# Two-layer convolution kernel: where the sines are computed, how the last channels of the first image are stored, and how the last image's tail is queued

## The chip, the cores and the metric

The kernel runs on one core of one Trainium2 chip. The metric is the device time of one execution in microseconds (us). Lower is better. Times of several runs are given as a median with their range.

## The reference, cut to what matters

The input x holds 8 images of 8 channels and 512 x 512 pixels in 32-bit floats. Two residual layers follow each other. Both normalise x over groups of two channels first.

```python
x = x + _L0_conv_ref(_gn(x), T, X, weights1_ri, weights2_ri)
x = x + _L1_conv_ref(_gn(x), K_local, Wp, bp, Wu, bu, Wg1, bg1, Wg2, bg2)
```

Layer 0 is spectral: it takes 32 low frequencies (8 in one direction, 4 in the other) of every second pixel, mixes the channels, and builds the image again from cosines and sines (`E1`, `E2`) whose arguments come from the vectors X and T. Layer 1 has three parts on its normalised input x:

```python
grid = drive                                    # drive = x
for _ in range(15):
    mapped = R * grid * (1.0 - grid)            # logistic map
    local = _conv(mapped, K_local, groups=8)    # 3x3, each channel by itself
    grid = 0.85 * (0.7 * mapped + 0.3 * local) + 0.15 * drive
cml_out = clip(grid, 0.0001, 0.9999)
nca_out = sigmoid(_conv(relu(_conv(x, Wp, bp)), Wu, bu))     # 3x3 to 128, 1x1 to 8
gin = concatenate([x, cml_out, nca_out])
g = sigmoid(_conv(relu(_conv(gin, Wg1, bg1)), Wg2, bg2))     # 3x3, 1x1
return g * cml_out + (1.0 - g) * nca_out
```

## The kernel before, in words

**Stages of an image.** The program calls an image an element. `layer0` (line 321) is a generator that does layer 0 and the normalisation of layer 1 in small pieces; each `yield` names the slot of the schedule in which the next piece may be put (wide, early, fill, late). It ends with `close` (line 414), which normalises a pair of channels and stores them to the DRAM plane `xn`. From `xn` three users read:

- `Slabs` and `Tail`: the 15 steps of the logistic map. A set is a tile of 128 partitions x 4 x 512. Each step is 48 matmuls from `convolve` (line 529), a VectorE addition (line 548) and a ScalarE square (line 554). Nine sets make an image: four for channels 0 to 3, four for channels 4 to 7, and the tail. Results go to the plane `cml`.
- `Hidden` (line 706): the 3x3 convolution to 128 channels, in 128 rounds of four image rows. A round is 24 matmuls (line 734) into four PSUM banks, which ScalarE empties for one half (line 740) and VectorE for the other (line 742). Its input tile `cols` serves four rounds and has two buffers; `Hidden.load` (line 714) issues the next one after every fourth round. `point` (line 757) does the 1x1 convolution; after every fourth round the result `y` goes to the plane `nca` (line 776), 16 rows at a time.
- `Gate` (line 783): 43 blocks of 12 rows. `load` (line 789) issues six DMAs (three for `gin`, three for `mix`), `conv` (line 806) needs 24 matmuls (line 811), a GpSimd subtraction (line 816), and two VectorE operations (lines 817 and 821). `point` (line 823) needs 6 matmuls (line 828), a sigmoid on ScalarE (line 832) and a GpSimd product (line 834). `finish` (line 836) adds on VectorE (line 839) and stores to `out` (line 846).

**Order.** Nothing is planned by a cost model. The order of the source is the order on every engine: `keep_order` (line 103) ties each instruction to the one before it on its engine. The unit of the schedule is a turn (line 1071), counted by `now`; `later(1, ...)` puts work off to the end of the turn. One turn, in `work` (line 1026), is: three map steps; `others.finish()` for the gates whose point was issued in the turn before; the transfers; up to three hidden rounds; the 1x1 sums; up to two gate convolutions; their points; the loads of new gates. While image b is mapped and convolved, the gates of image b-1 and layer 0 of image b+1 fill the gaps.

**The start.** Line 186 issues the loads of the eight channels of image 0. The loop of line 1004 then runs the pieces of its layer 0. At the piece with number 8, so after the statistics of all eight channels, it calls `sines` (line 224: three times a chain of seven VectorE instructions on 8 x 512 and a sine on ScalarE, then four small DMAs from ScalarE's queue) and `bands` (line 258: the weights of the map, 120 small GpSimd instructions). All of ScalarE's loads of constants and the stores of zero rows (lines 973 and 976) stand ahead of this in ScalarE's queue. As soon as four channels are stored, 16 loads (`first.load`, line 1018) of two of the four sets are issued. After the loop two `cols` loads follow (lines 1020 and 1021), and the other 16 set loads come from `Phase.fetch` (line 698) in the first turns. Eight rounds in three turns run before the first map step.

**The tail.** During the last image only 56 of its 128 rounds are done beside the map (line 54). What is left runs in the loop of line 1133: 72 rounds, three a turn, so 24 turns, and the 43 gates of this image. A turn loads two gates if at most four are loaded and waiting (line 1134). `Others.conv` (line 943) takes a gate if the turn has reached `hold` and the gate was loaded at least `lag` turns ago; line 1131 sets these to three turns from now and 2. In this tail the stores of `nca` go through GpSimd's queue, since `lag` is not 0 (line 776); the `cols` loads go through SyncE's queue (SP) like all other loads.

Of the kernel before, what the change touches and what calls it, by code (L numbers as in the profile page):

```python
# [41 lines left out]
P = 128  # L42
C = 8
N = 512
NS = N // 2
G = 4
# [19 lines left out]
assert TAIL_AT + TAIL_ROWS[0][1] == N - SLAB + TAIL_ROWS[1][0]  # L66
SLOTS, SHARED, MORE, LEAST = 19, 4, 7, 3
AHEAD = 12


MAGIC = 12582912.0
# [41 lines left out]
def view(t, offset, dims):  # L113

    return bass.AP(tensor=t.tensor, offset=t.offset + offset, ap=[list(d) for d in dims])
# [3 lines left out]
def conv_layers(ctx: ExitStack, tc: tile.TileContext, a, out):  # L119
    nc = tc.nc  # L120
# [42 lines left out]
    put_off, now = [], [0]  # L163

    def later(ticks, work):
        put_off.append((now[0] + ticks, work))
# [57 lines left out]
    def sines():  # L224
        u, k, t = (sets.take([8, N], name) for name in ("u", "k", "sines"))
        rd = sm.tile([8, 1], F32, name="rd")
        for to, name, col, shift in (
            (e1[:8], "X", 0, 0.25), (t, "X", 0, 0.0), (e2[:8], "T", 1, waves[:8, 2:3])
        ):
            xr = grid[name]  # L230
            nc.vector.tensor_tensor(rd, xr[:, 2:3], xr[:, 0:1], ALU.subtract)
            nc.vector.reciprocal(rd, rd)
            nc.vector.tensor_tensor(rd, rd, waves[:8, col : col + 1], ALU.mult)
            nc.vector.tensor_scalar(u, xr, rd, shift, ALU.mult, ALU.add)
            nc.vector.tensor_scalar(k, u, MAGIC, None, ALU.add)
            nc.vector.tensor_scalar(k, k, MAGIC, None, ALU.subtract)
            nc.vector.tensor_tensor(u, u, k, ALU.subtract)
            nc.scalar.activation(to, u, AF.Sin, scale=6.283185)
        nc.scalar.dma_start(out=e1[8:16], in_=t)
        for j in range(1, 4):  # L240
            nc.scalar.dma_start(out=e2[32 * j : 32 * j + 8], in_=e2[:8])
        for tile_ in (u, k, t, *grid.values()):
            sets.drop(tile_)
# [14 lines left out]
    def bands():  # L258
        nc.vector.tensor_scalar(kk, kk, -R * (1.0 - BETA) * EPS, None, ALU.mult)
        nc.vector.tensor_scalar(  # L260
            kk[:, 4::9], kk[:, 4::9], -R * (1.0 - BETA) * (1.0 - EPS), None, ALU.add
        )
        for c in range(C):
            for dx in range(3):
                to = band[:, c, dx]
                for dy in range(3):
                    at = c * 9 + dy * 3 + dx
                    nc.gpsimd.tensor_scalar(
                        part if dy else to, shift[:, dy], kk[:, at : at + 1], None, ALU.mult
                    )  # L270
                    if dy:
                        nc.gpsimd.tensor_tensor(to, to, part, ALU.add)
        ky = prep[:, 192 : 192 + C * 3].rearrange("p (c y) -> p c y", y=3)
        nc.vector.tensor_reduce(ky, kk.rearrange("p (c y x) -> p c y x", y=3, x=3), AX.X, ALU.add)
        full = prep[:, 224 : 224 + C]
        nc.vector.tensor_reduce(full, ky, AX.X, ALU.add)
        nc.vector.tensor_scalar(full, full, -0.25, -0.5, ALU.mult, ALU.add)
        nc.vector.tensor_scalar(ky, ky, 0.25, None, ALU.mult)
        nc.vector.tensor_copy(base[:, :, 1], full)
        for e, (j, dy) in enumerate(((0, 0), (2, 2), (3, 0), (4, 2))):  # L280
            nc.vector.scalar_tensor_tensor(
                base[:, :, j], ky[:, :, dy], ends[:, e : e + 1], full, ALU.mult, ALU.add
            )
        for c in range(C):
            at = slice(32 * (c % 4), 32 * (c % 4) + 32)
            nc.vector.tensor_copy(base_e[at, c // 4], base[at, c, 0:3])
        nc.vector.tensor_copy(base[64:, 0:4, 4], base[64:, 4:8, 4])
# [33 lines left out]
    def layer0(e, bank):  # L321
# [6 lines left out]
        for c in range(C):  # L328
            yield (LATE if c % 2 else EARLY), c
            xt = e.x[c]  # L330
# [61 lines left out]
        to = om[:16, :C]  # L392
# [21 lines left out]
        def close(g, mv):  # L414

            mean, rstd, std = yield from group_stats(mv, 1, bank)
            nc.vector.tensor_copy(means[:, 0, g : g + 1], mean)
            nc.vector.tensor_copy(means[:, 1, g : g + 1], std)
            for c in (2 * g, 2 * g + 1):
                xt = e.x[C + c]  # L420
                nc.vector.tensor_scalar(xt, xt, mean, rstd, ALU.subtract, ALU.mult)

                def store(c=c, xt=xt):
                    nc.sync.dma_start(
                        out=e.xn[1 : N + 1, c].rearrange("(p j) w -> p j w", j=4), in_=xt
                    )
                    e.done_with(C + c)
                    e.closed.append(c)

                later(1, store)  # L430

        def synthesis(ty, xt, half):
            ps, at = bank[-1], slice(2 * half, 2 * half + 2)
# [233 lines left out]
    class Phase:  # L667
# [23 lines left out]
        def squares(self, n):  # L691
            while self.squared < len(self.sets) and sets.room():
                if not self.ready(self.squared, 0, n + TICK):
                    break
                self.sets[self.squared].square()
                self.squared += 1

        def fetch(self, n):
            while n - self.at >= -AHEAD and self.loads:
                s, _, h = self.loads[0]  # L700
# [5 lines left out]
    class Hidden:  # L706
# [7 lines left out]
        def load(self):  # L714
            assert len(self.e.closed) == C
            t = wk.tile([P, 2, N], F32, tag="cols", name="cols", bufs=2)
            nc.sync.dma_start(
                out=t,
                in_=view(
                    self.e.xn, 16 * self.loaded * C * N, [[N, P], [2 * C * N, 2], [1, N]]  # L720
                ),
            )
            self.loaded += 1
            self.tiles.append(t)
# [58 lines left out]
    class Gate:  # L783
# [60 lines left out]
        def store(self):  # L844
            lo = self.first - self.r0
            nc.sync.dma_start(
                out=view(
                    out, self.e.b * C * N * N + self.first * N,
                    [[N, GR - lo], [N * N, C], [1, N]],
                ),  # L850
                in_=self.mix[C * lo : GR * C, 1],
            )
            shared.drop(self.mix)
# [115 lines left out]
    for i in range(3):  # L969
        xn = dram.tile([NP + 1, C, N], F32, name=f"xn{i}")  # L970
        cml, nca = (dram.tile([NP, C, N], F32, name=f"{name}{i}") for name in ("cml", "nca"))
        for plane in (xn, cml, nca):
            nc.scalar.dma_start(
                out=view(plane, 0, [[(NP - 1) * C * N, 2], [N, C], [1, N]]), in_=zrow
# [24 lines left out]
    e = element(0)  # L999
# [2 lines left out]
    turns = cycle(pairs)  # L1002
    others = Others()
    for n in count():
        if n == C:
            sines()
            bands()
        if not e.pieces:
            break
        ps = next(turns)  # L1010
        e.spectral(e.need[0], ps if e.need[0] == WIDE else ps[:, 0])
        tick()

        first = phases[0]
        while (
            len(e.closed) >= C // 2 and len(first.loads) > 8 * (SETS - 2) and sets.room()
        ):
            first.load()
    tick(end=True)
    e.hidden.load()  # L1020
    e.hidden.load()

    halves = pairs[:2], pairs[2:]
    used = [0]

    def work(steps, rounds, e, after, gates, transfers, squares=lambda: None):

        def half():
            used[0] += 1
            return halves[used[0] % 2]  # L1030

        settled = iter(())
        for n, (s, step) in enumerate(steps):
            ps = half()
            s.convolve(step, ps)
            next(settled, None)
            settled = s.settle(step, ps)
            next(settled)
            others.finish()
            if gates == 2:  # L1040
                others.load(1)
                gates = 1
        others.finish()
        transfers()
        for _ in range(rounds):
            e.hidden.round(half(), after, settled)
        next(settled, None)
        squares()


        first, second = halves[used[0] % 2], halves[(used[0] + 1) % 2]
        if not others.spectral(WIDE, second):
            used[0] += 1
            first, second = second, first
        groups = e.hidden.sums()
        if len(groups) == 2:
            e.hidden.point(groups.pop(0), first[1][:, 0])
        others.conv(first[0][:, 0])
        others.spectral(EARLY, [second[0][:, 0]])
        two = others.conv(second[0][:, 0])  # L1060
        if groups:
            e.hidden.point(groups[0], first[1][:, 1])
        others.spectral(FILL, [None])
        others.spectral(LATE, [second[1][:, 0], second[0][:, 0]])
        others.point()
        used[0] += two
        others.load(gates)
        tick()
        squares()
# [24 lines left out]
    for b in range(B):  # L1094
        e = elements[b]
# [3 lines left out]
        first, second = phases[2 * b : 2 * b + 2]  # L1099
# [28 lines left out]
        others.mapped.append(e)  # L1128


    others.after, others.hold, others.lag = None, now[0] + 3, 2
    sets.most = shared.most = SLOTS
    while e.hidden.n < ROUNDS or others.mapped or others.busy():
        turn(at, min(TICK, ROUNDS - e.hidden.n), e, None, 2 if len(others.loaded) <= 4 else 0)
# [57 lines left out]
```

## Time and profile before

| what | us |
|---|---|
| three runs, median (range) | 9339.16 (9327.55 to 9340.95) |
| profiled execution, its time | 9328.59 |
| profiled execution, its span | 9326.8 |
| first round of the hidden convolution begins | 138.0 |
| first map step begins | 175.4 |
| tail begins (first of its 24 turns) | 8838.3 |
| last hidden round's sums end | 9283.7 |
| last VectorE addition of a gate begins | 9322.1 |

Times inside the profile count from the start of the span. Engines are PE (matmul), PEld (its weight loads), DVE (VectorE), ACT (ScalarE), POOL (GpSimd) and SP (SyncE, which only issues DMAs here); a name with q is the engine's queue of instructions that issue or wait. In a row of groups the numbers behind the bar are busy time and mean nanoseconds of one, then the idle time just before and what ended it. In the timeline a bracket gives the idle time before the row and its releaser. In the table of stretches each engine has its busy time and number of instructions, then come TensorE's granted clock, the mean busy share of the 16 DMA engines and GB/s. PE is busy for 94% of the span, with the granted clock at 0.987 on average.

### The profile page before, as it was taken

The numbers are of one execution on the slowest core, as the hardware profiler recorded it, in microseconds if no ns is written. First come the engines' busy times: TensorE is split into PE (matmuls) and PEld (weight loads), VectorE is DVE, ScalarE is ACT, GpSimd is POOL, SyncE is SP. The second block draws the span as 40 slices with busy tenths as digits, with TensorE's granted clock in tenths as the row PEclk, the third lists the DMA queues.
The fourth block names the chain that finished last, engine by engine and source line by source line (L and its number), as shares of the span: only waits on it lengthen the run. The fifth ranks groups of instructions, "written<-read, shape, count | busy, mean of one in ns | idle before, by whom it ended". The sixth has DMA issues, their size and how long they took to land. (4 is left out here: it accounts for less than half of the span.)

```text
span 9326.8 us, 334742 instructions
## 1 busy us (share of the span) xinstructions
PE 8776.0 (94%) x150992; PEld 4165.1 (45%) x150992; DVE 5685.6 (61%) x5844; ACT 4101.0 (44%) x4285; POOL 3378.9 (36%) x4441
## 2 busy tenths in 40 slices
PE   5999999999999999999999999999999999899988
PEld 2445544444444444444444444444444444344433
DVE  5665567556665567655676556755567555555655
ACT  2445444444444444444444444444444444344422
POOL 3242334334343243433334343343433324453422
PEclk9999999999999999999999999999999999999999
DMA  5241356745566455754657546575455755665487
GB/s 158 79 127 39 96 150 167 171 109 152 148 178 146 112 155 145 184 137 112 169 146 176 129 108 167 156 179 126 111 158 167 173 117 129 144 153 119 105 212 184
DMA packets 697414, 1327.26 MB, mean 142 GB/s; under 512 B 146939, under 2 KB 152443, under 8 KB 668499
## 3 DMA queue, kind: packets, MB, share of 16 engines
q1 hardware_dynamic: 591840, 1244.38, 51.8%
q0 software_dynamic: 101792, 60.33, 3.0%
q8 instruction: 1187, 19.45, 0.9%
q14 instruction: 241, 1.97, 0.1%
q10 hardware_dynamic: 2354, 1.14, 0.0%
HBM read 977.48 MB, written 270.61 MB: 134 GB/s over the span
## 5 line engine op out<-in xcount | busy, mean ns | idle before, releaser
L535 PE MATMUL pair<-m,band 32*32 32x512 f32 x103680 | 3669.8, 605 | 205.2 <-issue 132.7
L554 ACT ACTIVATE m<-m 128x1024 f32<-128x1024 f32 x2016 | 2128.8, 1056 | 2081.0 <-DVE m L548 1994.9
L535 PEld LDWEIGHTS pair<-m,band 32*32 32x32 f32 x103680 | 2166.3, 103 | 1664.5 <-issue 820.3
L734 PE MATMUL pair<-cols,w_p 32*128 32x511 f32 (+1 forms) x24576 | 2800.1, 596 | 64.3 <-DMA cols<-xn 36.0
L734 PEld LDWEIGHTS pair<-cols,w_p 32*128 32x128 f32 x24576 | 1311.0, 185 | 1565.4 <-issue 1189.8
L548 DVE SCALAR_TENSOR_TENSOR m<-pair,dO 128x1024 f32<-128x1024 f32 x1152 | 1356.9, 1219 | 1040.0 <-PE pair L535 772.5
L581 POOL DMA_DIRECT2D m<-m x1568 | 855.3, 545 | 3061.0 <-ACT m L554 2983.1
L742 DVE TENSOR_SCALAR h<-pair,b_p 128x1024 f32<-128x1024 f32 x1024 | 1311.9, 1283 | 1045.4 <-PE pair L734 1035.3
L548 DVE SCALAR_TENSOR_TENSOR m<-pair,dE 128x1024 f32<-128x1024 f32 x1008 | 1187.3, 1219 | 867.3 <-PE pair L535 635.3
L740 ACT ACTIVATE h<-pair,b_p 128x1024 f32<-128x1024 f32 x1024 | 1141.2, 1115 | 1206.6 <-PE pair L734 1196.6
L834 POOL TENSOR_TENSOR mix<-mix 96x512 f32<-96x512 f32 x344 | 451.0, 1317 | 2010.8 <-ACT mix L832 1958.3
L761 PE MATMUL pair<-h,w_u 128*32 128x512 f32 x8192 | 999.0, 597 | 56.9 <-DVE y L770 30.4
L811 PE MATMUL pair<-gin,w_g 128*32 128x511 f32 (+1 forms) x8256 | 963.2, 604 | 64.5 <-DMA gin<-nca 45.8
L582 POOL DMA_DIRECT2D m<-m x1568 | 840.5, 536 | 36.7 <-issue 30.7
L811 PEld LDWEIGHTS pair<-gin,w_g 128*32 128x32 f32 x8256 | 254.3, 111 | 721.2 <-issue 654.8
L761 PEld LDWEIGHTS pair<-h,w_u 128*32 128x32 f32 x8192 | 246.2, 110 | 674.6 <-issue 516.5
L816 POOL TENSOR_TENSOR mix<-mix 96x512 f32<-96x512 f32 x344 | 446.4, 1300 | 191.0 <-DMA mix<-nca 143.5
L773 ACT ACTIVATE y<-y,b_u 128x512 f32<-128x512 f32 x256 | 184.9, 722 | 748.2 <-DVE y L770 747.9
L768 ACT COPY y<-pair 128x512 f32<-128x512 f32 x256 | 149.9, 586 | 693.3 <-PE pair L761 686.0
L558 POOL TENSOR_SCALAR dO<-dO 128x2048 f32<-128x2048 f32 x72 | 398.1, 5529 | 88.1 <-DVE m L548 87.0
L817 DVE SCALAR_TENSOR_TENSOR mix<-mix,back 96x512 f32<-96x512 f32 x344 | 379.7, 1104 | 81.0 <-DMA mix<-nca 63.9
L821 DVE TENSOR_SCALAR mix<-pair,b_g 128x512 f32<-128x512 f32 x344 | 257.2, 748 | 248.2 <-PE pair L811 238.2
(91 smaller groups left out, 3023.6 us busy)
## 6 DMA issues: line engine op xcount, KB each, us to landing
gin<-xn SPq DMA_DIRECT2D x344, 384.0 KB
cols<-xn SPq DMA_DIRECT2D x256, 512.0 KB
x<-in_x SPq DMA_DIRECT2D x120, 1024.0 KB
gin<-cml SPq DMA_DIRECT2D x344, 320.0 KB
gin<-nca SPq DMA_DIRECT2D x344, 320.0 KB
dE<-xn SPq DMA_DIRECT2D x288, 256.0 KB
dO<-xn SPq DMA_DIRECT2D x288, 256.0 KB
mix<-xn SPq DMA_DIRECT2D x344, 192.0 KB
```

The source lines that it names most:

```text
L535: nc.tensor.matmul(ps[h // 2][32 * t : 32 * t + 32, h % 2], band[at, self.channel(step - 1, h, t), dx], m[at, t, dx : dx + N], start=(n == ...
L548: nc.vector.scalar_tensor_tensor(u[:, at], ps[q], FLOOR, d[:, at], ALU.max, ALU.add)
L554: nc.scalar.square(u[:, at], u[:, at])
L581: nc.gpsimd.dma_start(out=view(tb, rb, dims), in_=view(ta, ra, dims))
L582: nc.gpsimd.dma_start(out=view(ta, ra + s, dims), in_=view(tb, rb + s, dims))
L734: nc.tensor.matmul(ps[g // 2][:, g % 2, lo:hi], w_p[p, dx, i % 2], self.cols[p, i // 2, at : at + hi - lo], start=(n == 0), stop=(n == 2), ...
L740: nc.scalar.activation(h[:, :2], ps[0], AF.Relu, bias=b_p)
L742: nc.vector.tensor_scalar(h[:, 2:], ps[1], b_p, 0.0, ALU.add, ALU.max)
L761: nc.tensor.matmul(ps[32 * g : 32 * g + 32], w_u[:, r % 4], h[:, g], start=(r == hs[0][0]), stop=(r == hs[-1][0]), tile_position=(0, 32 * g),)
L811: nc.tensor.matmul(ps[32 * j : 32 * j + 32, lo:hi], gband[:, dx], gin[:, j, at : at + hi - lo], start=(n == 0), stop=(n == 2), tile_positi ...
L816: nc.gpsimd.tensor_tensor(d, d, ng, ALU.subtract)
L834: nc.gpsimd.tensor_tensor(d, d, mix[: GR * C, 2], ALU.mult)
```

## The change

1. `sines()` moves from piece 8 to piece 3 of the loop of line 1004, so between the statistics of the third and the fourth channel; `bands()` moves from piece 8 to piece 5.
2. `close` makes one `store` for a pair of channels. For the last pair of image 0 this store moves only the top 16 partitions (64 image rows), which is what the first three `cols` tiles read of these channels. The other 112 partitions (`rest`) are stored after the two `cols` loads and after all 16 remaining set loads, which are now issued in one go.
3. In the tail `Hidden.load` issues its `cols` loads from GpSimd's queue. This applies while `others.lag` is not 0.
4. In `work`, `others.finish()` stands behind the rounds when the turn has no map steps, which is so in the tail.
5. In the tail `hold` grows from three turns to four and `lag` from 2 to 3. The condition for loading (at most four gates waiting) stays.

```diff
@@ -66,6 +66,7 @@
 SLOTS, SHARED, MORE, LEAST = 19, 4, 7, 3
 AHEAD = 12
+TOP = 16
@@ -416,18 +417,30 @@
-            for c in (2 * g, 2 * g + 1):
+            pair = (2 * g, 2 * g + 1)
+            for c in pair:
                 xt = e.x[C + c]
                 nc.vector.tensor_scalar(xt, xt, mean, rstd, ALU.subtract, ALU.mult)
 
-                def store(c=c, xt=xt):
-                    nc.sync.dma_start(
-                        out=e.xn[1 : N + 1, c].rearrange("(p j) w -> p j w", j=4), in_=xt
-                    )
+            def rows(lo, hi):
+                for c in pair:
+                    to = e.xn[1 : N + 1, c].rearrange("(p j) w -> p j w", j=4)
+                    nc.sync.dma_start(out=to[lo:hi], in_=e.x[C + c][lo:hi])
+
+            def rest(lo=TOP):
+                rows(lo, P)
+                for c in pair:
                     e.done_with(C + c)
-                    e.closed.append(c)
-
-                later(1, store)
+
+            def store():
+                if e.b == 0 and g == G - 1:
+                    rows(0, TOP)
+                    e.rest = rest
+                else:
+                    rest(0)
+                e.closed.extend(pair)
+
+            later(1, store)
@@ -714,7 +727,7 @@
             t = wk.tile([P, 2, N], F32, tag="cols", name="cols", bufs=2)
-            nc.sync.dma_start(
+            (nc.gpsimd if others.lag else nc.sync).dma_start(
                 out=t,
@@ -1002,8 +1015,9 @@
     for n in count():
-        if n == C:
+        if n == 3:
             sines()
+        if n == 5:
             bands()
@@ -1019,6 +1033,9 @@
     e.hidden.load()
     e.hidden.load()
+    while first.loads:
+        first.load()
+    e.rest()
@@ -1040,11 +1057,13 @@
                 gates = 1
-        others.finish()
+        if steps:
+            others.finish()
         transfers()
         for _ in range(rounds):
             e.hidden.round(half(), after, settled)
         next(settled, None)
+        others.finish()
         squares()
@@ -1128,7 +1147,7 @@
-    others.after, others.hold, others.lag = None, now[0] + 3, 2
+    others.after, others.hold, others.lag = None, now[0] + 4, 3
     sets.most = shared.most = SLOTS
```

## The prediction, made before the changed kernel ran

> **What bounds the kernel now.** I read busy times first: PE is busy 94% of the span at a granted clock of 0.987, so the middle has little to give and no edit touches it. The edits act in the first 175 us and after 8838, so I read those stretches. First, the chain of waits through one turn of the tail:
>
> ```profile
> 9028.33 0.69 ACT mix L832
> ...
> 9029.09 1.27 POOL mix L834
> ...
> 9030.42 1.63 issue
> 9032.05 3.11 DVE mix L839
> 9035.16 1.21 DVE h L742
> ...
> 9036.41 2.84 PE pair L734 x20
> ```
>
> PE's third round (x20) waits for VectorE's `h`, which queued behind the gates' L839, which waited for GpSimd's L834 of the turn before. The engine with the work waits because of the order on another one.
>
> Next the timeline at the tail's start, where the longest PE stall of the tail stands:
>
> ```profile
> 8857.14 1.34 SPq L796 DMA_DIRECT2D gin<-xn  x1
> ...
> 8874.83 0.38 SPq L717 DMA_DIRECT2D cols<-xn  x1
> ...
> 8886.55 4.58 PE L734 MATMUL pair<-cols,w_p 32*128 32x512 f32 x24 [16.50 <-DMA cols<-xn]
> ```
>
> The `cols` load stood behind twelve gate loads on SP: 17.7 us between first gate load and `cols`, then 11.7 to landing.
>
> Then the table of stretches: a turn with two gates and no finish ahead of its rounds, one with both, and the drain after the last round.
>
> ```profile
> 8894.90:8912.90 18.00, 17.60 (x160) 6.32 (x156) 7.36 (x8) 5.25 (x7) 3.01 (x3) 1.00 0.90 203
> 8912.90:8932.70 19.80, 18.70 (x160) 6.62 (x160) 11.24 (x9) 5.16 (x6) 5.51 (x6) 1.00 0.88 213
> ...
> 9289.00:9326.00 37.00, 19.03 (x120) 4.87 (x112) 13.19 (x13) 3.42 (x5) 13.92 (x11) 0.83 0.61 157
> ```
>
> 18.0 against 19.8 is the price of the finish. In the drain PE works half the time; the timeline names the transfers:
>
> ```profile
> 9297.38 5.34 PE L811 MATMUL pair<-gin,w_g 128*32 128x512 f32 x24 [5.84 <-DMA gin<-nca]
> ...
> 9312.97 4.47 PE L811 MATMUL pair<-gin,w_g 128*32 128x512 f32 x24 [5.00 <-DMA gin<-nca]
> ```
>
> Last, the start. ScalarE computes nothing before 27.5 us, and the first round waits for stores:
>
> ```profile
> 27.50 1.28 ACT L343 ACT_TABLE_LOAD   x1 [27.50 <-DMA nca<-zrow]
> ...
> 116.59 7.20 SPq L424 DMA_DIRECT2D xn<-x  x4
> ...
> 134.54 0.91 SPq L717 DMA_DIRECT2D cols<-xn  x2
> ...
> 138.01 9.81 PE L734 MATMUL pair<-cols,w_p 32*128 32x512 f32 x72 [19.46 <-DMA cols<-xn]
> ```
>
> **What the Trainium skill says.** (1) "SBUF — State Buffer", Who interferes with whom: a VectorE instruction with two SBUF inputs excludes a GpSimd one that reads SBUF. The trace agrees: L839 takes 0.74 us alone, 1.74 or 3.1 beside GpSimd's L816. (2) "DMA: Bandwidth & Descriptors", Issuing engines are not separate DMA queues: another issuer saves only issue time, the 16 engines are shared. So edit 3 can remove a place in a queue, not bytes; no run here shows a `cols` load by GpSimd. (3) Same page, SWDGE vs HWDGE vs iDMA: the two kinds feed different queues of a DMA engine, served in turn, so such a load need not wait for SP's backlog. The `nca` stores by GpSimd (256 KB, 0.57 us of issue) landed in 7.1 us at the median, 8.8 at most.
>
> **The change part by part.** Sums are against the profiled span, 9326.8.
>
> *Sines and bands.* 24 VectorE instructions, three sines, four ScalarE DMAs and one table load move ahead of channel 3. VectorE reaches them at 17.0. The first chain takes 2.9 us; the second overwrites `u`, so it waits for the first sine, and that stands behind ScalarE's DMAs (27.5), a table load 1.28, three copies 0.5, a second table load 1.28, the sine 0.63: 31.2. Two more chains of 2.1, a sine between and the last hand-over end at 36.2. Five channels' statistics at 2.48, bands 3.56 (its 120 GpSimd instructions run beside), the aggregate 1.05: 53.2. The mean's copy follows 0.9 later, 54.1 against 52.2 before. **Cost 1.9 us**, where idle VectorE time seemed free. If the sine came early it would gain up to 8; I keep -8 and +3 as ends.
>
> *Top rows first.* The DMA engines are full from 99 to 133: set loads to 122.5, then 4.2 MB of stores at about 409 GB/s, so `cols` goes at 134.5. With the shift set loads end at 124.4; 2.1 MB for channels 4 and 5 and 0.26 MB of top rows take 5.8, and landing 1.1: `cols` at 131.3. **Net start gain 3.2 us** (the 1.9 is inside). The 16 set loads (4.2 MB at 230 GB/s, 18 us) and `rest` (1.8 MB, 4.5 us) then lie beside rounds that last to 175, and the third `cols` tile, behind them on SP, is used at 185. If that cover went, up to 10 us would come back; the high end takes some of it.
>
> *Cols by GpSimd.* The first such load is free at 8852 and needed at 8870. GpSimd is idle then, and DMA share is 0.30 up to 8861. It lands in 7.1 to 17.6 us (one store's median, twice its maximum, being twice the bytes; I take 11.7 as SP's did), so by 8864. **Gain 16.5**, and 1.9 of the 4.58 us round after it, slow at a granted clock of 0.75. What is late next: the 2.5 us wait for ScalarE before it, which stays. Later loads: while `cols` waits for its round on GpSimd, L816 and L834 of this turn and the `nca` store stand behind; ScalarE's L832 needs L816, but only some 17 us into the turn. Taken at nothing; each turn in four whose L816 falls beside L839 may lose up to 1.5.
>
> *Finish behind rounds.* Two L839 go behind the third `h`, where VectorE has 3.7 us of idle time waiting for gate matmuls (0.76, 1.17 and 1.75 in the 18.0 us turn). At 0.74 each they fit; at 3.5 together they still meet L828. From 8912.9 to 9225.0 sixteen turns take 19.51 on average, so **1.5 us a turn** goes. SP's `out` stores, and the gate loads behind them, start some 6 us later in the turn; gates have three turns to land.
>
> *Lag 3.* Counted by the loading condition: turns 0, 1, 2 load two gates each, six wait, turn 3 loads none and, by `hold`, convolves none. From turn 4 a cycle of four repeats: two, two, two, none. So 30 gates are convolved in the 24 turns where 38 were, and 13 remain, not 5; 7 of them are not even loaded (before 2).
>
> *Sum.* Turn 3 starts at 8894.9 - 18.4 = 8876.5. A turn without gates takes 11.3 (turns 0 and 1: 10.6 and 12.0): 8887.8. Then 15 x 18.0 and 5 x 11.3: the rounds end at 9214.3 (before 9283.7). In the drain nine gates' loads follow each other from 1.5 us before: per gate 7.8 us (two PE waits, 9297.4 and 9313.0, two gates apart) plus 0.5 for its store: 74.7. Then 13.8 from the last landing to the end, as before. 13 gates of PE work (3.5 each) are shorter, 46. End: 9214.3 - 1.5 + 74.7 + 13.8 = 9301.3; less 3.2: **9298.1, a gain of 28.7 us**, 0.31%. The profiled time was 1.8 above its span; its 9328.6 is 10.6 below the median, so I carry the difference over: 9339.2 - 28.7 = 9310.
>
> **The rivals.**
> - *The drain runs faster:* with 7.2 us a gate (228 GB/s, between the tail's 213 and 232) and residual stalls gone: 9 gates save 10 us, 15 turns at 17.6 (PE's busy time in the 18.0 us turn) another 6: 9294, and 9285 with the early sine. For: share 0.61 there. Against: SP issues a gate's loads only as earlier ones land.
> - *Transfers set the tail, no change:* 43 gates at 1.84 MB with their stores, 16 `cols` at 0.52 and 18 `nca` at 0.26 make 92 MB from 8857 to the last landing at 9313, 202 GB/s. At that rate they end as before whatever PE does: 9331 in the profile, 9343 as median. For: DMA share 0.88, and the first six gates took 9.7 us each. Against: no gate matmul between 8903 and 9283 waited for a transfer, and the mean includes idle DMA (74 GB/s from 9240 to 9258).
> - *Slower:* 16 `cols` loads by GpSimd land late. Slack is four rounds and what lies between: 20 us in gated turns, 13.2 where a turn without gates intervenes. At 22 us landing twelve loads lose 2 and four 8.8: 59 us, 9369. It decides from about 21 us. For: the full engines. Against: 8.8 at most for half the bytes.
>
> That edits 3 to 5 do nothing is excluded: they change the source order, which every engine keeps.
>
> **How the numbers follow.** Forecast 0.55 (9295 to 9324 by itself: 7.4 to 9 us a gate, 0 to 1 us more per gated turn, start -8 to +3), fast drain 0.17, no change 0.15, slower 0.13. Measurement tells about 0.2%, or 19 us, from no change: faster 0.70 (all of the drain's and nearly all of the forecast's), same 0.17, slower 0.13. The range, 9287 to 9340, leaves out the slower case and the edge of the fast one.
>
> **What would show it.** Right: VectorE idle from about 20 to 31 us before the second chain; the mean's copy near 54; `cols` near 131; no 16 us wait near 8870; turns of 18.0; rounds ending near 9214, then 13 gates in some 87 us, PE waiting for `gin`. Wrong: the mean's copy before 50, `cols` landing in over 15 us, turns of 19 or more, or a drain under 75 or over 100 us.

## The result, and the profile after

The changed kernel takes 9297.9 us (median of 14 runs, 9273.36 to 9319.84), against 9337.2 us for the kernel before beside it (14 runs, 9315.62 to 9345.87). The ratio is 0.996, with a 95% interval from 0.995 to 0.997: a gain of 28 to 47 us. The prediction was 9310 us and its range 9287 to 9340.

The profiled execution of the changed kernel took 9319.84 us, the slowest of its 14, with a span of 9318.1 us. That is only 8.7 us below the span of before, so the spans have to be cut into stages first. Here "start" ends with the first map step, "tail" begins with the first of its 24 turns, and "rounds" end with the last matmul of the hidden convolution (its sums end 2.6 us later).

| kernel | span | start | middle | tail | of it rounds | of it drain |
|---|---|---|---|---|---|---|
| before | 9326.8 | 175.4 | 8662.9 | 488.5 | 442.7 | 45.8 |
| changed | 9318.1 | 173.3 | 8680.9 | 463.9 | 364.9 | 99.0 |

The edits act in the start (-2.1) and in the tail (-24.6). The middle, where the work is the same, was 18.0 us longer in this one execution. The ten other kernels below give middles of 8642 to 8670 us, 8657 on average, with no pattern in their edits. The middle is therefore spread between executions, and the medians, not the two spans, carry the result. Lines behind `close` have numbers 13 higher in the changed kernel (734 is now 747, 816 is 829, 839 is 852).

The start, from the timeline of the changed kernel (start, duration, engine and line; the bracket holds the idle time before, and who ended it):

```profile
27.59 1.28 ACT L344 ACT_TABLE_LOAD   x1 [27.59 <-DMA nca<-zrow]
...
31.30 0.47 DVE L235 TENSOR_SCALAR u<-X,rd 8x512 f32<-8x512 f32 x1 [11.28 <-ACT e L239]
...
53.22 0.16 DVE L310 COPY mean<-pair 128x4 f32<-128x4 f32 x1 [0.56 <-PE pair L304]
...
131.46 0.91 SPq L730 DMA_DIRECT2D cols<-xn  x2
...
134.91 5.34 PE L747 MATMUL pair<-cols,w_p 32*128 32x512 f32 x24 [15.22 <-DMA cols<-xn]
```

VectorE stands idle for 11.28 us before the second chain, because ScalarE is still issuing zero-row stores. The mean's copy comes at 53.2, and the first round at 134.9 instead of 138.0.

The tail's start, from the same timeline, where the 16.5 us wait for `cols` stood before:

```profile
8868.05 0.76 POOL L730 DMA_DIRECT2D cols<-xn  x1 [45.80 <-PE pair L747]
...
8883.80 7.11 PE L747 MATMUL pair<-cols,w_p 32*128 32x512 f32 x44 [3.24 <-ACT y L781]
```

GpSimd issues the load as soon as its buffer is free. What is late next is the wait for ScalarE's `y`, 3.24 us here and 2.52 before. The 16 `cols` loads that GpSimd issues landed like this:

```profile
DMA to landing us min/median/max: 3.9/9.0/10.8
```

The table of stretches, the turns with gates and then the drain:

```profile
8905.40:9219.10 313.70, 313.70 (x2804) 115.87 (x2802) 145.46 (x162) 105.80 (x119) 92.37 (x88) 1.00 0.84 211
...
9221.70:9318.10 96.40, 58.47 (x394) 16.12 (x386) 45.61 (x41) 9.60 (x14) 35.38 (x27) 0.84 0.76 192
```

PE is busy in all of the 313.7 us: in this stretch of the rounds it waits for nothing. In the drain it works 58 of 96 us, and the first matmuls of eight gates wait for a load of `gin`, 27.4 us in all. Two of them:

```profile
9243.68 4.27 PE L824 MATMUL pair<-gin,w_g 128*32 128x512 f32 x24 [2.81 <-DMA gin<-nca]
...
9306.11 2.78 PE L824 MATMUL pair<-gin,w_g 128*32 128x512 f32 x24 [2.29 <-DMA gin<-nca]
```

These two are seven gates apart: 62.4 / 7 = 8.9 us a gate. The waits put the limit of the drain at the transfers, but the DMA engines are busy only 76% of it: whether their rate sets the 8.9 us, or the moment at which SP can issue a gate's loads, wasn't tried.

### The profile page after: what moved, and what is told of

Same layout as the page of the kernel before. It is cut to its first block, busy times and chain, and to the rows that moved or that the text cites. A ratio compares the mean times of both kernels' runs of the same rounds, so it can differ in the third digit from the quotient of the medians.

```text
span 9318.1 us, 334845 instructions
## 1 busy us (share of the span) xinstructions
PE 8769.9 (94%) x150992; PEld 4156.6 (45%) x150992; DVE 5641.0 (61%) x5844; ACT 4100.2 (44%) x4285; POOL 3388.2 (36%) x4457
## 3 DMA queue, kind: packets, MB, share of 16 engines
q1 hardware_dynamic: 587520, 1235.99, 51.4%
## 5 line engine op out<-in xcount | busy, mean ns | idle before, releaser
L774 PE MATMUL pair<-h,w_u 128*32 128x512 f32 x8192 | 999.7, 598 | 56.6 <-DVE y L783 30.4
L829 POOL TENSOR_TENSOR mix<-mix 96x512 f32<-96x512 f32 x344 | 446.0, 1299 | 214.1 <-DMA mix<-nca 138.4
L834 DVE TENSOR_SCALAR mix<-pair,b_g 128x512 f32<-128x512 f32 x344 | 257.1, 747 | 234.3 <-PE pair L824 224.4
```

What stands on the lines that cost most here:

```text
L774: nc.tensor.matmul(ps[32 * g : 32 * g + 32], w_u[:, r % 4], h[:, g], start=(r == hs[0][0]), stop=(r == hs[-1][0]), tile_position=(0, 32 * g),)
L829: nc.gpsimd.tensor_tensor(d, d, ng, ALU.subtract)
```

## The experiments

Stages are in us, from each kernel's profile; ratios are to the kernel before beside it.

| kernel | median | ratio (95%) | start | middle | tail | rounds | drain |
|---|---|---|---|---|---|---|---|
| edits 3 to 5 alone | 9295.6 | 0.9963 [0.9950, 0.9976] | 176.3 | 8642.3 | 460.6 | 364.6 | 96.0 |
| edits 1 and 2 alone | 9319.1 | 0.9992 [0.9983, 1.0000] | 172.3 | 8666.2 | 492.0 | 445.1 | 46.9 |
| edit 5 undone | 9306.7 | 0.9973 [0.9965, 0.9981] | 173.4 | 8668.3 | 472.0 | 419.5 | 52.5 |
| six gates may wait | 9289.3 | 0.9955 [0.9940, 0.9970] | 172.7 | 8669.4 | 455.5 | 404.1 | 51.4 |
| edit 3 undone | 9317.8 | 0.9984 [0.9976, 0.9992] | 171.1 | 8657.1 | 477.4 | 379.4 | 98.0 |
| edit 4 undone | 9301.6 | 0.9969 [0.9958, 0.9981] | 172.9 | 8654.5 | 456.9 | 368.9 | 88.0 |
| edits 3 and 4 undone | 9323.5 | 0.9988 [0.9977, 0.9998] | 173.5 | 8646.5 | 482.3 | 392.7 | 89.6 |
| early sines undone | 9290.3 | 0.9954 [0.9943, 0.9966] | 172.1 | 8652.2 | 467.4 | 366.3 | 101.1 |
| zero rows later, six gates | 9280.5 | 0.9943 [0.9928, 0.9959] | 163.7 | 8670.2 | 454.5 | 401.9 | 52.6 |
| the same, sines late | 9288.1 | 0.9960 [0.9946, 0.9973] | 174.2 | 8645.1 | 455.9 | 405.1 | 50.8 |

Each row's stages come from one profile, so the spread has to be known before two rows are compared. Seven kernels have edits 1 and 2 and the zero rows in their old place: their starts run from 171.1 to 173.5. Three have the same tail edits (the changed kernel, edits 3 to 5 alone, early sines undone): their tails run from 460.6 to 467.4, their rounds from 364.6 to 366.3, their drains from 96.0 to 101.1. A difference within these spreads is not read as an effect.

**Which half pays.** The start edits and the tail edits, each alone. In the first kernel:

```diff
-        if n == 3:
+        if n == C:
             sines()
-        if n == 5:
             bands()
...
-    while first.loads:
-        first.load()
-    e.rest()
```

> The kernel before with edits 3 to 5 alone (cols by GpSimd, finish behind the rounds, lag 3); the start is as before. Theory (two ends, added up): the first map step begins at 175.4 as before, and from the first turn of the tail to the end it takes 464 us as in the changed kernel (488.5 before): 24 us less than before, 0.26%. Rival (the start edits also shift the middle for the better, since the medians are 39 us apart and the two ends of the profiles only 27): the same tail, but the other 15 us go with the start edits.

> The kernel before with edits 1 and 2 alone (sines and bands early, top rows first); the tail is as before. Theory: the first map step begins at 173.3, 2.1 us earlier than before, the tail takes 488 us, and the median is 2 us below before, which timing cannot tell from no change. Rival (the start edits shift the middle): 10 to 15 us below before.

The tail edits alone give a tail of 460.6 us and the ratio of the whole change. The start edits alone take the start to 172.3 and leave the tail as it was (492.0); their ratio can hardly be told from no change. The gain is the tail's, as far as timing tells. The 10 to 15 us that a rival gave to the start edits lie within the interval of their own kernel (0 to 16 us), but the tail edits reach the whole ratio without them.

**Lag 3.** Edit 5 undone, and then, with edit 5 kept, more gates allowed to wait:

```diff
-    others.after, others.hold, others.lag = None, now[0] + 4, 3
+    others.after, others.hold, others.lag = None, now[0] + 3, 2
```

> The changed kernel with edit 5 undone (hold three turns, lag 2), so two gates in nearly every turn of the tail, 38 of 43 beside the rounds. Theory (transfers set the tail: 92 MB at some 215 GB/s, whatever the order): PE now waits for gin inside the rounds, the rounds end later by about the 8 gates moved back (28 us of PE work) plus waits, the drain takes some 45 to 60 us instead of 96, and the tail as a whole is within 15 us of 464. Rival (lag 3 is what costs, since 13 gates are left for a drain bound by transfers): no waits for gin in the rounds, tail 439 us, 25 us less. Second rival (lag 3 gives the time in which gates land): PE waits of several us in every turn, tail 475 or more.

```diff
-        turn(at, min(TICK, ROUNDS - e.hidden.n), e, None, 2 if len(others.loaded) <= 4 else 0)
+        turn(at, min(TICK, ROUNDS - e.hidden.n), e, None, 2 if len(others.loaded) <= 6 else 0)
```

> The changed kernel with one number changed: a turn of the tail loads two gates if at most six wait, not four, so that loads never pause; by count 37 gates are convolved beside the rounds and 6 remain (13 in the changed kernel). Theory (transfers set the tail, and the pause of one turn in four leaves DMA share at 0.84): DMA share rises above 0.88 in the rounds, the drain shrinks to 45 to 60 us, the tail takes 440 to 455 us. Rival (the DMA engines are full at 0.85 already): same tail, 464, PE waiting in the rounds for what it no longer waits for in the drain.

Without edit 5 the rounds take 54.6 us longer and the drain 46.5 less: the tail moves by 8.1 us of 464, just more than its spread, and the two ratios have intervals that overlap. A stretch beside the rounds, and PE's longest group of waits from the tail's start to the end of the rounds, first with edit 5 undone:

```profile
8893.00:9260.00 367.00, 346.01 (x3012) 125.26 (x3008) 175.27 (x186) 110.26 (x127) 113.35 (x102) 0.99 0.84 210
...
PE pair L824 <- DMA gin<-nca: 13.5, 7, 3.1
```

and with six gates:

```profile
8893.00:9246.00 353.00, 341.96 (x3022) 123.90 (x3013) 170.13 (x184) 109.79 (x126) 113.39 (x103) 1.00 0.87 219
...
PE pair L824 <- DMA gin<-nca: 5.5, 2, 3.9
```

The transfers run at 84% and 210 GB/s in one, as in the changed kernel (84%, 211), and at 87% and 219 in the other, short of the 88% expected. With edit 5 undone PE waits for `gin<-nca` 13.5 us beside the rounds and 17.1 in the drain. With edit 5 it has no such wait beside the rounds and waits 27.4 us for `gin` in the drain. So with edit 5 PE sets the pace beside the rounds and the transfers that of the drain; without it the transfers also take part in the rounds. They don't set them alone: 38 gates and not 30 are convolved there, and at 3.5 us a gate (half the difference between a turn with two gates, 17.55, and one without, 10.64) the eight more account for some 28 of the 54.6 us, by estimate. Six waiting gates take 8.4 us off the tail (455.5); the two kernels below that have them too give 454.5 and 455.9, so this stands clear of the spread.

**Cols by GpSimd, and the finish behind the rounds.** Edit 3 undone, edit 4 undone, and both:

```diff
-            (nc.gpsimd if others.lag else nc.sync).dma_start(
+            nc.sync.dma_start(
```

> The changed kernel with edit 3 undone: the cols loads of the tail go through SP again. Theory (the place in SP's queue is what cost): PE's wait for cols near the tail's start comes back with 15 to 18 us, and since every later load is tied to the turns, the rounds end 16 to 20 us later and the tail takes 480 to 484 us. Rival (transfers set the tail): the wait comes back, but the drain shortens by about as much, and the tail stays within 5 us of 464. Second rival: later cols loads wait too, behind the out stores that now stand later in the turn; several waits of some us, 490 or more.

```diff
-        if steps:
-            others.finish()
+        others.finish()
         transfers()
...
-        others.finish()
         squares()
```

> The changed kernel with edit 4 undone: the gates of the turn before are finished ahead of the rounds. Theory: a turn with two gates takes 19.1 us again, not 17.55, fifteen times, so the rounds take 388 us, not 365, the drain stays at 96 to 99, and the tail takes 484 to 488 us. Rival (transfers set the tail): the rounds lengthen, but the drain shortens as far, since loads go on meanwhile: 464 to 470 us.

With edit 3 undone, the wait for `cols` is back:

```profile
PE pair L747 <- DMA cols<-xn: 15.1, 1, 15.1
```

The rounds take 14.5 us longer and the tail 477.4 us, a little less than the 480 to 484 expected. The ratio goes from 0.996 to 0.9984, which is some 20 us. With edit 4 undone, the expectation failed: the rounds were only 4.0 us longer, turns with two gates stayed at 17.55 us but for the last one, and the tail took 456.9 us. The timeline of that kernel shows the reason:

```profile
8915.46 2.49 POOL L847 TENSOR_TENSOR mix<-mix 96x512 f32<-96x512 f32 x2 [11.09 <-ACT mix L845]
...
8916.75 2.40 DVE L852 SCALAR_TENSOR_TENSOR mix<-mix,back 96x512 f32<-96x512 f32 x2 [3.84 <-POOL mix L847]
8917.90 0.59 POOL L789 DMA_DIRECT2D nca<-y  x1
...
8919.08 1.27 DVE L755 TENSOR_SCALAR h<-pair,b_p 128x1024 f32<-128x1024 f32 x1
...
8921.21 0.72 POOL L730 DMA_DIRECT2D cols<-xn  x1 [2.73 <-DMA gin<-xn]
...
8921.95 2.51 POOL L829 TENSOR_TENSOR mix<-mix 96x512 f32<-96x512 f32 x2
```

The finish step (L852) again stands ahead of `h`, but its two additions take 2.40 us. GpSimd's subtractions (L829), which used to run beside them, now stand behind the `cols` load on GpSimd's queue. That load waits until 8921, and by then L852 has long ended. (The row names a landing of `gin`; for the other 15 of these loads the profile names PE's matmuls of the rounds, which read the buffer that the load needs.) So edit 3 by itself pulls the two engines apart. The same trace has a control. GpSimd issues the last `cols` load of the tail at 9154.23, and the next turn with two gates has none:

```profile
9169.90 4.78 DVE L852 SCALAR_TENSOR_TENSOR mix<-mix,back 96x512 f32<-96x512 f32 x2 [3.85 <-POOL mix L847]
...
9171.63 2.50 POOL L829 TENSOR_TENSOR mix<-mix 96x512 f32<-96x512 f32 x2
...
9175.93 2.84 PE L747 MATMUL pair<-cols,w_p 32*128 32x512 f32 x20 [1.09 <-DVE h L755]
```

Here L829 follows at once, two L852 take 4.78 us, PE waits for `h`, and the turn takes 19.75 us. These 2.2 us are more than half of the 4.0; the rest arises before the first gate. If that is right, undoing both brings the collision back in every cycle:

> The changed kernel with edits 3 and 4 both undone: the cols loads issued by SP again, the finish step ahead of the rounds again, the lag of 3 and the start edits kept. The question is who removed the wait of PE for VectorE's h in turns with two gates, which came back with neither edit undone alone (17.55 us a turn in both). Theory (the two edits are redundant: the load's wait on GpSimd's queue spaces the subtraction from L852, or L852 stands behind h; either suffices): turns with two gates and a preceding finish return to 19 to 19.5 us, PE waits for VectorE's h some 10 us or more in all, two L852 take 4 us or more beside L829, and the rounds end some 370 + 15 + 10 to 25 = 393 to 410 us after the tail's start, the tail about 485 to 500. Rival (the lag of 3 removes it): turns stay near 17.6, PE waits for h 1 us in all, rounds about 379 to 385 as with the cols loads alone on SP, the tail 475 to 480.

It does. The timeline of that kernel:

```profile
8967.76 2.48 POOL L847 TENSOR_TENSOR mix<-mix 96x512 f32<-96x512 f32 x2 [12.58 <-ACT mix L845]
...
8969.05 3.41 DVE L852 SCALAR_TENSOR_TENSOR mix<-mix,back 96x512 f32<-96x512 f32 x2 [4.70 <-POOL mix L847]
8970.20 3.39 POOL L829 TENSOR_TENSOR mix<-mix 96x512 f32<-96x512 f32 x2
8972.39 2.46 DVE L755 TENSOR_SCALAR h<-pair,b_p 128x1024 f32<-128x1024 f32 x2
```

L829 overlaps L852 again, both are slow, and two `h` follow each other without a pause because the first was late. The group L852 in the turns of the rounds (busy time, mean ns), in this kernel:

```profile
L852 DVE SCALAR_TENSOR_TENSOR mix<-mix,back 96x512 f32<-96x512 f32 x30 | 52.9, 1802 | 57.6 <-POOL mix L847 57.6
```

with edit 4 alone undone:

```profile
L852 DVE SCALAR_TENSOR_TENSOR mix<-mix,back 96x512 f32<-96x512 f32 x32 | 41.9, 1346 | 59.6 <-POOL mix L847 59.6
```

and in the changed kernel:

```profile
L852 DVE SCALAR_TENSOR_TENSOR mix<-mix,back 96x512 f32<-96x512 f32 x28 | 19.6, 740 | 0.0
```

740 ns is its time alone. The Trainium skill says in "SBUF — State Buffer", Who interferes with whom, that a VectorE instruction with two SBUF inputs contends with a GpSimd one that reads SBUF. These three means agree with it. In each cycle of four one turn is 19.7 us long again and another 18.4, where either edit alone keeps them at 17.55, and the rounds are 13.3 us longer than with edit 3 alone undone. PE's waits with both undone:

```profile
PE pair L747 <- DVE h L755: 5.4, 5, 1.1
...
PEld pair L747 <- DVE h L755: 12.2, 10, 1.9
```

The size was less than expected on PE itself (5.4 us, not some 10; 12.2 us show at its weight loads), and the rounds (392.7 us) and the tail (482.3) fell just short of 393 to 410 and 485 to 500. Edit 4 (this kernel against the one with edit 3 alone undone) shortens the rounds by these 13.3 us and lengthens the drain by 8.4. The other pair goes the same way: 4.0 us less in the rounds, 11.0 more in the drain. Rounds that end sooner leave more transfers to the drain; edit 4 also starts the `out` stores later, and which of the two weighs more wasn't tried. The tail is even 7.0 us longer in the changed kernel than with edit 4 undone, about the spread of the tail. By time, the changed kernel and the one with edit 4 undone can't be told apart (0.996 and 0.9969, intervals that overlap).

**Where the start goes.** Sines and bands put back behind the eighth channel; then the zero-row stores taken out of the head of ScalarE's queue:

> The changed kernel with edit 1 undone: sines and bands after the eighth channel, top rows of the last channels still stored first. Theory (early sines wait for ScalarE's DMAs and cost about 1 us): the mean's copy comes back to 52.2 and the first map step begins at 171.5 to 172.5, not at 173.3. Rival (sines among the loads gain): the first map step begins at 175 or later. The tail is the changed kernel's, 464, and timing shows no difference.

In the next edit `zeros` is a function that issues the same twelve stores as the lines taken out:

```diff
-        for plane in (xn, cml, nca):
-            nc.scalar.dma_start(
-                out=view(plane, 0, [[(NP - 1) * C * N, 2], [N, C], [1, N]]), in_=zrow
-            )
-        nc.scalar.dma_start(out=xn[NP], in_=zrow[:C])
...
+        if n == C:
+            zeros()
```

> Two additions to the changed kernel: the twelve stores of zero rows leave ScalarE's queue ahead of the loop and are issued after the eighth channel; and a turn of the tail loads two gates if at most six wait. Theory: ScalarE is free from 14 us, the sines no longer hold up VectorE, the mean's copy comes at about 43 instead of 53, the first map step at about 163 to 165 instead of 173; the tail takes 455 us as in cap6. Together 18 us less than the changed kernel, 0.2%. Rival (the loads of x set the start anyway): the mean's copy at 50 or later, first map step at 171 or later.

> The changed kernel with the zero-row stores after the eighth channel, the cap at 6, and the sines and bands back behind the eighth channel. Theory (early sines pay once ScalarE is free: they fill VectorE's idle time among the first channels, while late ones stand on its path): the mean's copy near 52, the first map step near 172, some 8 us later than the 163.7 with early sines, and the time about 8 us above that version, 9288 or so. Rival (the zero rows' stores alone made the start early, since the first images' statistics run on ScalarE too): the mean's copy near 45, the first map step within 2 us of 164.

With late sines the mean's copy comes at 52.07 and the first map step 1.2 us sooner, so early sines cost about 1 us at the mean's copy (with early sines it came between 52.9 and 53.5 in six of seven profiles, at 51.4 in one). At the first map step 1.2 us lie within the spread. The tail of this kernel is 3.5 us longer than that of the changed one; its median, 9290.3, is no slower. With the zero rows behind the eighth channel's statistics, the same early sines pay:

```profile
13.98 1.28 ACT L344 ACT_TABLE_LOAD   x1 [13.98 <-issue]
...
21.71 0.47 DVE L235 TENSOR_SCALAR u<-X,rd 8x512 f32<-8x512 f32 x1 [1.60 <-ACT e L239]
...
43.62 0.16 DVE L310 COPY mean<-pair 128x4 f32<-128x4 f32 x1 [0.56 <-PE pair L304]
```

VectorE waits 1.60 us instead of 11.28, the mean's copy comes 9.6 us sooner, and the first map step, at 163.7, too. Not all of this comes from ScalarE being free. The loads of x go faster too: SP issues the last one at 17.6 us, not at 27.3, and between 20 and 30 us the DMA engines move 387 GB/s, not 264. Why the twelve stores slow these loads wasn't tried. With six waiting gates this kernel has the lowest ratio of all, 0.9943, but its interval overlaps that of six gates alone.

The last kernel was to show what early sines are worth once ScalarE is free. It told less than was meant. The mean's copy came at 47.66, which is 4.0 us later and between the two expectations. The other 6.5 us of the later start have a different cause:

```profile
47.25 0.63 ACTq L990 DMA_DIRECT2D xn<-zrow  x1
...
54.40 1.28 ACT L317 ACT_TABLE_LOAD   x1 [9.60 <-DMA nca<-zrow]
...
55.99 0.18 DVE L319 RECIPROCAL rstd<-std 128x4 f32<-128x4 f32 x1 [7.46 <-ACT std L317]
```

With the sines late, the zero-row stores followed them in ScalarE's queue and stood ahead of the standard deviation (L317), for which VectorE then waited 7.46 us (0.79 with early sines). Early sines are thus worth 4.0 us at the mean's copy once the zero rows stand later. Moving the zero rows is worth 4.4 us there with late sines (52.07 to 47.66) and 9.6 with early ones. Late sines with the zero rows elsewhere weren't tried.

## Why the prediction was right

- **Sines.** The chain of causes held: VectorE idle until 31.30 (said: 31.2), mean's copy at 53.2. The cost was 1.0 us, not 1.9, since the copy came 0.9 us sooner than the sum had it. An early sine, for which the prediction kept a gain of up to 8 us, is worth 4.0 us where ScalarE is free; the 8.6 us between that kernel's copy and the one before also hold the 4.4 us that moving the zero rows brings with late sines.
- **Top rows.** `cols` went at 131.46 (131.3 said). The first map step gained 2.1 us, not 3.2: of the 3.1 us at the first round, 1.0 was lost in the eight rounds that follow.
- **Cols by GpSimd.** Right in its mechanism, and the largest part, but too large by some us: undoing it costs 13.5 us in the tail (the prediction added 16.5 for the wait and 1.9 for the slow round after it). Turns 0 to 2 take 40.5 us instead of 56.6, which is 16.1 less and not 18.4. The wait for `y` that was to stay grew by 0.7 us, and the matmuls after it are slow in their turn: 44 take 7.11 us at a granted clock of 0.76, where 72 take 8.00 at 1.00. So the 1.9 us were not gained. (The 0.75 that the prediction gives its slow round is the mean from 8861.0 to 8894.9, idle time and all; in the 4.58 us themselves it was 0.61.) Loads landed in 9.0 us at the median, 10.8 at most, so the slower rival, which needs 21, was far off. The Trainium skill's "DMA: Bandwidth & Descriptors", Issuing engines are not separate DMA queues, agrees on the bytes: beside the rounds the share of the DMA engines was 0.84 with edit 3 and without it (211 and 205 GB/s). What was gained was a place in the queue. The page calls the time to initiate a DMA usually small; here twelve loads ahead in SP's queue took 17.7 us to be issued.
- **Finish behind rounds.** This step failed in its cause. The prediction gave the 1.5 us a turn to edit 4, and took what edit 3 queues on GpSimd "at nothing". In fact that queueing removes the collision too. Each edit alone keeps the turn at 17.5 us; edit 4 on top of edit 3 takes 4.0 us off the rounds, and the drain grows by more than that. That the sum for these turns came out all the same is luck: an edit that was priced at nothing here did the work. One reading was off as well: in the trace of before, L839's 1.74 us stood beside L834, the product, and only its 3.1 us beside L816.
- **Lag 3 and the sizes.** The counted pattern (two, two, two, none) and the 30 gates beside the rounds came as said. Turns with two gates took 17.55 us, not 18.0, because the stalls in the 18.0 us turn that served as the price vanished too; turns without took 10.6, not 11.3. By the sums, the rounds ended after 367.5 us and not 376. The drain took 96.4 and not 87, since a gate took 8.9 us and not 8.3: the table of stretches has 192 GB/s over all of it. The two misses (-8.5 and +9.4) cancel, as they would where transfers hold the end: rounds that PE ends sooner leave more of them. The prediction didn't count on this, so a tail of 463.9 us where its sum has 463.0 is in part luck.
- **The sum.** -2.1 and -24.6 make -26.7 us, against the -28.7 of the prediction. The median fell by 39. The remaining 12 us are not explained by the two stages. The interval (28 to 47 us) begins 1 us above their sum, and the tail alone spreads over 7 us between profiles; whether the edits shorten the middle a little isn't settled, since one profile of each kernel doesn't tell.
- **The rivals.** "Transfers set the tail" named the right limit for the drain, and with edit 5 undone for part of the rounds. But it took the 202 GB/s of before for a fixed rate, and beside the rounds 200 to 219 were reached. The fast drain (7.2 us a gate) was not seen.

## What to carry to other kernels

When two edits are each said to remove the same collision, undo them one at a time and together; where either one is enough, the gain belongs to neither alone. Where the transfers of a stretch are near their limit, count what moves from one stage to the next as returned, and price an edit by the whole chain of stages, not by the one it shortens. Before moving compute ahead to fill an idle engine, read what its partner engine still has to issue.

## What was not expected of the hardware

- A waiting DMA on GpSimd's queue acts as a spacer for the arithmetic behind it: the `cols` load waited 2.73 us and kept L829 away from L852, which ran at 1346 ns in the mean instead of 1802. In the one turn without such a load two L852 took 4.78 us instead of 2.40.
- On ScalarE twelve zero-row stores hold back its arithmetic for some 7 us (47.25 to 54.40), 0.43 to 0.63 us each, and it computed nothing between them. At the head of the kernel they hold it back by 13.6 us (27.59 instead of 13.98), and the loads of x on SP run slower beside them (264 instead of 387 GB/s from 20 to 30 us).
- The same middle, with the same instructions, took from 8642 to 8681 us in twelve profiles: 0.4%, as much as the whole gain.
